# Filter transfers in thirds, networks in three pieces, and A's last Haar products behind C's first pieces

## The chip, the cores and the metric

One core of one Trainium2 chip (the record numbers the chips of the three batches of experiments 1, 3 and 4; each batch has its own runs of the kernel before). The time is the device time of one launch in microseconds (us), given as the median of several runs. Every run told of here was in the fast state, and every kernel's result agreed with the reference. The engines: PE is TensorE, PEld its weight loads, DVE VectorE, ACT ScalarE, POOL GpSimd, SP the engine that issues the transfers. Half clock means that the profile shows a granted clock of PE of 0.5.

## The reference, cut to what matters

Four layers in fp32 on x of (4, 64, 256, 256). Layers 0, 2 and 3 are long convolutions whose filters come from a small network; layer 1 mixes channels in the Haar domain.

```python
def implicit_filter(z, ...):                 # z: 256 positions x 33
    h = sin(freq * (z @ w1 + b1)); h = sin(freq * (h @ w2 + b2)); h = sin(freq * (h @ w3 + b3))
    return (h @ wo) * decay                  # 256 x 64: one filter of 256 taps per channel
def conv(x, ...):                            # layers 0, 2, 3
    hx, hy = implicit_filter(... X ...), implicit_filter(... Y ...)
    k = outer product of hx and hy per channel
    y = irfft2(rfft2(x, 512) * rfft2(k, 512) / 512)[..., :256, :256]   # a causal 2-D convolution
    return y + x * bias[:, None, None]
def haar_layer(x, v, conv_w, tau):           # layer 1
    f = haar2d(x)
    acc = sum_i soft_threshold(einsum("bchw,oc->bohw", f * v[i], conv_w[i]), tau[i])    # i = 0, 1
    return haar2d(acc, inverse=True) + x
```

## The kernel before

The filter is an outer product, so each convolution is a Toeplitz product along the rows and one along the columns. The program has three phases on two groups of two images. **A** is layer 0 and the forward Haar transform; its coefficients go to DRAM (`coef`). **B** mixes them and stores `mixed`. **C** is the inverse Haar transform and layers 2 and 3. B reads the coefficients back into `ft`, mixes them on PE (into a tile that is called `f` too) and thresholds them through `m`; in C the inverse Haar transform goes through `ci`, whose products with a Haar matrix on PE are `c1ps` and give `cz`; the row and column products of layer 2 are `c1r` and `c1c`, those of layer 3 `c2r` and `c2c`. A has 64 rounds of 12 pieces; in a round PE does four products with rows (`a1ps`), four with columns (`a2ps`) and the Haar products of the round before (`a3ps`). PE's schedule is the program's order; other engines receive their work in that order too.

A Toeplitz tile is read from DRAM. For that each filter is written 24 times, padded with zeros to a period of 384, into `filt`. This is `spread`: for one layer and one quarter of the channels, two DMAs (X filter, Y filter) of 16 source rows each.

```python
PERIOD, REPEATS = N + P, 24            # 384 elements, 1536 bytes a repeat
...
    def network(ls):                   # the networks of the layers ls, as pieces
        def front(d):
            ...                        # one matmul and one eviction to u per layer
            nc.vector.tensor_scalar(k, u, INV_2PI, ROUND, ALU.mult, ALU.add)
            nc.vector.tensor_scalar(k, k, ROUND, None, ALU.subtract)
            for c in (C1, C2, C3):
                nc.vector.scalar_tensor_tensor(u, k, -c, u, ALU.mult, ALU.add)
            nc.vector.tensor_scalar(u, u, PI, -PI, ALU.min, ALU.max)
        def back():
            nc.scalar.activation(st["h"], st["u"], AF.Sin)
        ...
        for d in range(3):
            pieces += [lambda d=d: front(d), back]
    ...
    def spread(l, q):
        begin = q * QUARTER if (l, q) != (0, 0) else FIRST * CI
        for w in range(2):
            s = slice(w * C + begin, w * C + (q + 1) * QUARTER)     # 16 rows
            src = filters[l][s].unsqueeze(1)
            nc.sync.dma_start(filt[l][s], src.to_broadcast([src.shape[0], REPEATS, PERIOD]))
    ...
    rest = [load_tau] + [lambda q=q: spread(0, q) for q in range(1, 4)]
    rest.append(...)                                                # weights of two networks
    rest += network([1, 2])
    rest += [lambda l=l, q=q: spread(l, q) for l in (1, 2) for q in range(4)]
    rest.append(scale_tau)
```

The list `rest` lies beside the first 32 rounds of A, evenly over its pieces:

```python
    def beside(main, side, lead, tail):
        done = 0
        for k, p in enumerate(main):
            p()
            want = len(side) * max(0, k + 1 - lead) // max(1, len(main) - lead - tail)
            for q in side[done:want]:
                q()
            done = max(done, want)
    ...
    beside(a[:cut_a], rest, 2, 3 * M)                               # M = 4
```

The end of a round's data: GpSimd makes the Haar transform along the free axis into `fw`; PE multiplies half of it by a Haar matrix (`product`) and transposes the other half, which DVE transforms (in tiles `t`; from round 31 on PE multiplies all of it); ACT moves the products to `f`. `f` has two buffers, and its stores go to `coef`. All transfers are issued by SP.

```python
        def product(t, j):
            if j == 0:
                s["f"] = big("out", f"f_{t}", 2)      # two buffers
            ...
            later(lambda: nc.scalar.activation(dst, ps, AF.Copy, scale=wcol_sb[:, m : m + 1]))
        def store(t):
            for e in range(CI):
                nc.sync.dma_start(coef[grp][c0 + e], src)            # 512 KB each
```

A meets C here. `a_last[0]` is the rest of GpSimd's work on the last round, `a_last[1:M+1]` its Haar products, `c_first` the first inverse Haar products, and `c[:M]` the first row products (`c1r`) of C.

```python
    beside(a[-6 * M : -2 * M], c_before[:1], 2 * M, M)
    beside(a[-2 * M :], c_before[1:], 0, 0)           # first inverse Haar of C, on DVE
    main = a_last[:1] + c_first
    for pair in zip(c[:M], a_last[1:]):
        main += pair
    main += a_last[M + 1 :] + c[M:cut_c]
    beside(main, phase_b(1), 5 * M, 0)
```

Of the kernel before, what the change touches and what calls it, by code (L numbers as in the profile page):

```python
# [48 lines left out]
PERIOD = N + P  # L49
REPEATS = 24  # L50
# [6 lines left out]
M = CI * NB  # L57
# [15 lines left out]
def conv_haar_kernel(  # L73
    ctx: ExitStack, tc: tile.TileContext, x, zT, w1, wbd, cols, decay, wo_first, decay_first, bias, haarW, haarH, ident, wcol, wrow, mixT, v, tau, out
):
    nc = tc.nc
# [8 lines left out]
    filt = [dram.tile([P, REPEATS, PERIOD], F32, tag=f"filt{l}", name=f"filt{l}") for l in range(NL)]  # L85
# [26 lines left out]
    def load_toeplitz(l, t, bufs):  # L112


        tiles = []
        for e in range(CI):
            c = t % ROUNDS * CI + e
            tile_ = image("toep", f"toep{l}_{t}_{e}", bufs)
            for w in range(2):
                start = (w * C + c) * REPEATS * PERIOD  # L120
                src = bass.AP(filt[l].tensor, filt[l].offset + start, [[PERIOD - 8, 16], [PERIOD - 1, 8], [1, N]])
                nc.sync.dma_start(tile_[:, w, :], src)
            tiles.append(tile_)
        return tiles
# [8 lines left out]
    def constant(name, src, shape):  # L133
        t = mp.tile(shape, F32, tag=name, name=f"{name}_sb")
        nc.sync.dma_start(t, src)
        return t
# [9 lines left out]
    def network(ls):  # L146

        n = len(ls)
        st = {}

        def part(name, width=N, bufs=1):
            return mp.tile([P, n, width], F32, tag=f"{name}{n}", name=f"{name}{ls[0]}", bufs=bufs)

        def front(d):
            ps = mps.tile([P, n, N], F32, tag="ps", name=f"mlp_ps{ls[0]}{d}")
            u, k = part("u"), part("k")
            for e, l in enumerate(ls):
                if d == 0:
                    nc.tensor.matmul(ps[:, e, :], w1_sb[:, l, :], z_sb[:, l, :], start=True, stop=True)
                else:  # L160
                    nc.tensor.matmul(ps[:, e, :], wbd_sb[l][:, d - 1, :], st["h"][:, e, :], start=True, stop=True)
            for e, l in enumerate(ls):
                nc.vector.tensor_scalar(
                    u[:, e, :], ps[:, e, :], cols_sb[:, l, d : d + 1], cols_sb[:, l, 3:4], ALU.add, ALU.mult
                )

            nc.vector.tensor_scalar(k, u, INV_2PI, ROUND, ALU.mult, ALU.add)
            nc.vector.tensor_scalar(k, k, ROUND, None, ALU.subtract)
            for c in (C1, C2, C3):
                nc.vector.scalar_tensor_tensor(u, k, -c, u, ALU.mult, ALU.add)  # L170
            nc.vector.tensor_scalar(u, u, PI, -PI, ALU.min, ALU.max)
            st["u"] = u

        def back():
            st["h"] = part("h", bufs=2)
            nc.scalar.activation(st["h"], st["u"], AF.Sin)

        def repeated(r):

            ps = mps.tile([4 * REPEATS, N], F32, tag="ps", name=f"mlp_first{r}")  # L180
            nc.tensor.matmul(ps, wo_first_sb[:, r], st["h"][:, 0], start=True, stop=True)
            t = repeats[r]
            nc.vector.tensor_tensor(t[:, :N], ps, decay_first_sb[:, r], ALU.mult)
            for w in range(2):
                to = filt[0][w * C + r * CI : w * C + (r + 1) * CI].rearrange("c r e -> (c r) e")
                nc.sync.dma_start(to, t[w * CI * REPEATS : (w + 1) * CI * REPEATS])


        def last():
            ps = mps.tile([P, n, N], F32, tag="ps", name=f"mlp_out{ls[0]}")  # L190
            for e, l in enumerate(ls):
                nc.tensor.matmul(ps[:, e, :], wbd_sb[l][:, 2, :], st["h"][:, e, :], start=True, stop=True)
            padded = part("padded", PERIOD)
            nc.vector.memset(padded, 0.0)
            for e, l in enumerate(ls):
                nc.vector.tensor_tensor(padded[:, e, :N], ps[:, e, :], decay_sb, ALU.mult)
                filters[l] = padded[:, e, :]

        pieces = []
        for d in range(3):  # L200
            pieces += [lambda d=d: front(d), back]
        if ls == [0]:
            pieces += [lambda r=r: repeated(r) for r in range(FIRST)]
            pieces += [lambda r=r: first_toep.append(load_toeplitz(0, r, 4 * CI)) for r in range(FIRST)]
        return pieces + [last]
# [5 lines left out]
        nc.gpsimd.memset(t, 0.0)  # L211
    QUARTER = C // 4

    def spread(l, q):

        begin = q * QUARTER if (l, q) != (0, 0) else FIRST * CI
        for w in range(2):
            s = slice(w * C + begin, w * C + (q + 1) * QUARTER)
            src = filters[l][s].unsqueeze(1)
            nc.sync.dma_start(filt[l][s], src.to_broadcast([src.shape[0], REPEATS, PERIOD]))  # L220

    thresholds = []

# [27 lines left out]
    for p in network([0]):  # L251
        p()

    rest = [load_tau] + [lambda q=q: spread(0, q) for q in range(1, 4)]
    rest.append(lambda: wbd_sb.extend(constant(f"wbd{l}", wbd[:, l], [P, 3, P]) for l in (1, 2)))
    rest += network([1, 2])
    rest += [lambda l=l, q=q: spread(l, q) for l in (1, 2) for q in range(4)]
    rest.append(scale_tau)

    def toeplitz(ps, data, t, which):  # L260
# [61 lines left out]
    def phase_a():  # L322
# [138 lines left out]
        def piece(t, j):  # L461
            flush()
            if j == 0:
                if t == 0:
                    load(0)
                    load(1)
                    spread(0, 0)
                load(t + 2)
            if j < M:
                rows(t, j)  # L470
                if t > 0:
                    run(st[t - 1]["ops"], 2)
            elif j < 2 * M:
                columns(t, j - M)
                if j == M and t > 1:
                    coarsest(t - 2)
                if j == M + 2 and t > 1 + paired:
                    store(t - 2)
            else:
                if j == 2 * M and 1 < t <= 1 + paired:  # L480
                    store(t - 2)
                if t > 0:
                    product(t - 1, j - 2 * M)
                if t < total - 1:
                    run(st[t]["ops"], 2)
            if j == 3 * M - 1 and 0 < t <= paired:
                run(st[t - 1]["pair"], 2)
            if j < 2 * M and 1 < t <= 1 + paired:
                run(st[t - 2]["pair"], 2)
# [284 lines left out]
# [10 lines that stand above are left out]
    (a, a_last), (c_before, c_first, c) = phase_a(), phase_c()  # L784
    cut_a, cut_c = ROUNDS * 3 * M, (ROUNDS - 2) * 4 * M
# [6 lines left out]
    beside(a[cut_a : -6 * M], phase_b(0), 5 * M, 0)  # L792
    beside(a[-6 * M : -2 * M], c_before[:1], 2 * M, M)
    beside(a[-2 * M :], c_before[1:], 0, 0)
    main = a_last[:1] + c_first
    for pair in zip(c[:M], a_last[1:]):
        main += pair
    main += a_last[M + 1 :] + c[M:cut_c]
    beside(main, phase_b(1), 5 * M, 0)
    during.close()  # L800
    wp = pool("w", 2)
# [109 lines left out]
```

## Time and profile before

The median of four runs is 2908.59 us (2906.88 to 2909.84); the profiled run's span is 2905.2 us. The rows below take the start of a round as its first `a1ps` matmul in the timeline. An undisturbed round of this phase is 13.14 us long, or 14.00 us when it also holds matmuls of a network; from round 31 on, with all Haar products on PE, it takes about 14.05 us (rounds 32 and 33).

| stretch of PE's time, before | us | lost in it |
|---|---|---|
| start to the first A matmul | 23.5 | not touched |
| rounds 0 to 7 | 107.0 | first transfers, layer 0 |
| rounds 8 to 17 | 140.4 | 5.5 over 10 x 13.14 and four network matmuls of 0.87 |
| rounds 18 to 33 | 233.0 | rounds 25, 28 and 31 took 19.5, 21.0 and 19.9 |
| rounds 34 to 61, beside group 0's mixing | 651.0 | not touched |
| round 62 to the first `c2r` matmul | 55.5 | wait for `fw`, half clock |
| the rest (C, group 1's mixing) | 1694.7 | not touched |

The view that the prediction leaves out is that of the transfers. These are before's while the filters of layers 1 and 2 are written; the columns of the last two lines are the tile, the number of DMAs, the size of one and the median time from issue to landing. The first two lines are forty equal slices of the window: tenths of busy time of the 16 DMA engines, and what they moved.

```profile
DMA  7998899889999988887899989998879998899887
GB/s 279 262 154 154 248 261 328 110 130 274 330 314 146 141 270 274 140 165 181 271 340 331 144 113 210 296 196 130 142 262 267 371 242 119 127 316 270 138 165 221
...
coef<-f SPq DMA_DIRECT2D x23, 512.0 KB, 12.2
filt<-padded SPq DMA_DIRECT2D x16, 576.0 KB, 8.4
```

Read the first line against the second. The engines are busy everywhere, yet eight times the rate falls to between 110 and 165 GB/s: eight pairs of filter transfers. A busy engine isn't a fast one.

### The profile page before, as it was taken

How to read it: one execution, taken by the hardware profiler on the slowest of the kernel's cores; microseconds unless marked ns; L12 is line 12 of the kernel's file. 1: busy time of each engine (PE TensorE's matmuls, PEld its weight loads, DVE VectorE, ACT ScalarE, POOL GpSimd, SP SyncE). 2: the span in 40 equal slices, each digit the busy share in tenths (PEclk: the TensorE clock that was granted, in tenths of full speed). 3: DMA queues.
4: the chain of work that ended last, by engine and by line, in shares of the span. 5: the costliest groups of instructions: out<-in, count | busy, mean ns of one | idle time of the engine just before them, and what ended most of it. 6: DMA issues, size and time to landing. Idle time of an engine off the chain costs nothing.

```text
span 2905.2 us, 46908 instructions
## 1 busy us (share of the span) xinstructions
PE 2837.1 (98%) x16428; PEld 2413.6 (83%) x16428; DVE 1968.5 (68%) x3461; ACT 1141.9 (39%) x1731; POOL 1955.6 (67%) x2486
## 2 busy tenths in 40 slices
PE   7999989999999999999999999999999999999999
PEld 6989978777777777888888888888899999999998
DVE  4577643888888887377777777777755666656665
ACT  2344333555555555344444444444422122221221
POOL 4777766888888888666676676676684455544550
PEclk9999999999999999999999999999999999999999
DMA  7966998999999997686777777777644444444442
GB/s 194 231 202 199 214 221 245 340 327 318 319 309 326 323 312 270 217 279 225 262 263 240 259 250 259 241 257 257 209 144 150 146 135 131 137 149 147 135 131 80
DMA packets 372697, 657.66 MB, mean 226 GB/s; under 512 B 33742, under 2 KB 273775, under 8 KB 372464
## 3 DMA queue, kind: packets, MB, share of 16 engines
q1 hardware_dynamic: 372464, 654.67, 70.0%
q8 instruction: 132, 2.16, 0.3%
q14 instruction: 101, 0.83, 0.1%
HBM read 438.53 MB, written 216.01 MB: 225 GB/s over the span
## 4 chain that ended last, share of the span: by engine, by line
PE 81%; DVE 6%; DMA 4%; POOL 3%; issue 3%; ACT 2%; SPq 0%; DVEq 0%; POOLq 0%; ACTq 0%
PE f L536 12%; PE c2c L264 8%; PE c1r L264 8%; PE c1c L264 8%; PE c2r L264 8%; PE a1ps L264 5%; PE a2ps L264 5%; PE c2c L265 4%; PE c2r L265 4%; PE c1c L265 4%; PE c1r L265 4%; PE a3ps L372 3%; PE a1ps L265 2%; PE a2ps L265 2%; PE wps L661 2%
## 5 line engine op out<-in xcount | busy, mean ns | idle before, releaser
L544 ACT ACTIVATE m<-f 128x1024 f32<-128x1024 f32 x256 | 262.2, 1024 | 639.3 <-DVE f L540 595.6
L536 PE MATMUL f<-ft,mix_sb 128*128 128x512 f32 x1024 | 489.2, 600 | 21.6 <-DVE m L554 21.0
L551 DVE TENSOR_TENSOR f<-f,tau 128x1024 f32<-128x1024 f32 x256 | 314.9, 1230 | 166.0 <-ACT f L547 166.0
L559 POOL TENSOR_TENSOR m<-m,ft 128x1024 f32<-128x1024 f32 x128 | 302.2, 2361 | 179.5 <-DVE m L554 179.0
L562 POOL TENSOR_TENSOR gt<-m,m 128x1024 f32<-128x1024 f32 x128 | 302.1, 2360 | 157.4 <-DVE m L554 138.7
L540 DVE TENSOR_TENSOR f<-f,v 128x1024 f32<-128x1024 f32 x256 | 314.6, 1229 | 120.2 <-PE f L536 118.8
L264 PE MATMUL a1ps<-toep,x 128*128 128x256 f32 x1024 | 312.4, 387 | 17.7 <-ACT f L381 14.4
L554 DVE SCALAR_TENSOR_TENSOR m<-f,m 128x1024 f32<-128x1024 f32 x256 | 311.0, 1215 | 0.0
L264 PE MATMUL c2c<-toep,ch 128*128 128x256 f32 x1024 | 306.3, 381 | 0.0
L264 PE MATMUL a2ps<-toep,ay 128*128 128x256 f32 x1024 | 305.9, 381 | 0.1
L264 PE MATMUL c2r<-toep,cy 128*128 128x256 f32 x1024 | 305.8, 380 | 0.0
L264 PE MATMUL c1c<-toep,ch 128*128 128x256 f32 x1024 | 305.8, 380 | 0.0
L536 PEld LDWEIGHTS f<-ft,mix_sb 128*128 128x128 f32 x1024 | 174.5, 190 | 154.7 <-issue 122.4
L696 ACT COPY ch<-c2r 128x512 f32<-128x512 f32 x256 | 149.9, 588 | 357.6 <-PE c2r L265 356.6
L696 ACT COPY ch<-c1r 128x512 f32<-128x512 f32 x256 | 148.5, 589 | 328.2 <-PE c1r L265 328.1
L547 ACT ACTIVATE f<-f 128x1024 f32<-128x1024 f32 x256 | 263.0, 1027 | 0.0
L710 DVE SCALAR_TENSOR_TENSOR o<-cy,bias_sb,c2c 128x512 f32<-128x512 f32 x256 | 188.8, 742 | 71.1 <-PE c2c L265 64.7
L352 DVE SCALAR_TENSOR_TENSOR x<-x,bias_sb,a2ps 128x512 f32<-128x512 f32 x256 | 188.1, 743 | 65.0 <-PE a2ps L265 48.0
L299 POOL TENSOR_TENSOR i<-g 128x8 f32<-128x8 f32 x63 | 13.5, 215 | 322.3 <-DMA g<-mixed 322.2
L381 ACT ACTIVATE f<-a3ps,wcol_sb 128x512 f32<-128x512 f32 x196 | 130.7, 684 | 253.4 <-PE a3ps L372 145.0
L299 POOL TENSOR_TENSOR i<-i,g 128x16 f32<-128x16 f32 x378 | 205.9, 545 | 26.0
L273 POOL TENSOR_TENSOR fw<-x 128x1024 f32<-128x1024 f32 x64 | 121.2, 1894 | 148.9 <-DVE x L352 148.6
(97 smaller groups left out, 6600.1 us busy)
## 6 DMA issues: line engine op xcount, KB each, us to landing
toep<-filt SPq DMA_DIRECT2D x768, 128.0 KB, 3.4
x<-in_x SPq DMA_DIRECT2D x256, 256.0 KB, 6.1
coef<-f SPq DMA_DIRECT2D x128, 512.0 KB, 4.2
ft<-coef SPq DMA_DIRECT2D x128, 512.0 KB, 6.0
v<-in_v SPq DMA_DIRECT2D x128, 512.0 KB, 6.7
tau<-taus SPq DMA_DIRECT2D x128, 512.0 KB, 6.6
mixed<-gt SPq DMA_DIRECT2D x128, 512.0 KB, 4.9
g<-mixed SPq DMA_DIRECT2D x128, 512.0 KB, 6.3
```

The costliest lines, as they stand in the source:

```text
L264: nc.tensor.matmul(ps[:, m, :], data[:, 0, cut], t[:, which, :], start=True, stop=False)
L265: nc.tensor.matmul(ps[:, m, HALF:], data[:, 1, cut], t[:, which, :HALF], start=False, stop=True)
L299: engine.tensor_tensor(even, s, d, ALU.add)
L536: nc.tensor.matmul(un[u]["f4"][:, j, :], mix_sb[:, u % 2, :], f[:, j, :], start=True, stop=True)
L540: nc.vector.tensor_tensor(f4, f4, weights(st[u // 2]["v"], u % 2), ALU.mult)
L544: nc.scalar.activation(un[u]["m"], un[u]["f4"], AF.Sign)
L547: nc.scalar.activation(un[u]["f4"], un[u]["f4"], AF.Abs)
L551: nc.vector.tensor_tensor(f4, f4, weights(st[u // 2]["tau"], u % 2), ALU.subtract)
L554: nc.vector.scalar_tensor_tensor(un[u]["m"], un[u]["f4"], 0.0, un[u]["m"], ALU.max, ALU.mult)
L559: nc.gpsimd.tensor_tensor(m0, m0, data(st[s]["f"]), ALU.add)
L562: nc.gpsimd.tensor_tensor(data(st[s]["g"]), m0, un[2 * s + 1]["m"], ALU.add)
L696: later(lambda: nc.scalar.copy(y, ps))
```

## The change

Its intent: shorter bursts of filter traffic, so that the stores of `f` don't wait behind them; a network's arithmetic out of the way of DVE's evictions; and other work for PE while GpSimd finishes the last `fw`.

```diff
-        def front(d):
+        def product(d):
             ...                                  # matmuls, evictions to u
+            st["u"], st["k"] = u, k
+        def reduce():
+            u, k = st["u"], st["k"]
             nc.vector.tensor_scalar(k, u, INV_2PI, ROUND, ALU.mult, ALU.add)
             ...                                  # the other five instructions, as before
-        def back():
+        def sine():
             ...
-            pieces += [lambda d=d: front(d), back]
+            pieces += [lambda d=d: product(d), reduce, sine]
...
-    def spread(l, q):
+    def spread(l, q, part=slice(0, REPEATS)):
             ...
-            nc.sync.dma_start(filt[l][s], src.to_broadcast([src.shape[0], REPEATS, PERIOD]))
+            times = part.stop - part.start
+            nc.sync.dma_start(filt[l][s, part], src.to_broadcast([src.shape[0], times, PERIOD]))
...
-    rest = [load_tau] + [lambda q=q: spread(0, q) for q in range(1, 4)]
+    thirds = [slice(k, k + REPEATS // 3) for k in range(0, REPEATS, REPEATS // 3)]
+    rest = [load_tau] + [lambda q=q, k=k: spread(0, q, k) for q in range(1, 4) for k in thirds]
...
-    rest += [lambda l=l, q=q: spread(l, q) for l in (1, 2) for q in range(4)]
+    rest += [lambda l=l, q=q, k=k: spread(l, q, k) for l in (1, 2) for q in range(4) for k in thirds]
...
-    main = a_last[:1] + c_first
-    for pair in zip(c[:M], a_last[1:]):
+    main = a_last[:1] + c_first + c[:M]
+    for pair in zip(c[M : 2 * M], a_last[1:]):
         main += pair
-    main += a_last[M + 1 :] + c[M:cut_c]
+    main += a_last[M + 1 :] + c[2 * M : cut_c]
```

The list `rest` grows from 21 to 46 items, so the spacing changes with the size: the transfers not only get smaller, they also begin earlier. The two aren't the same cause, and the experiments take them apart.

More of the change, by code (lines that the diff above doesn't have):

```diff
@@ L171, in front @@
             nc.vector.tensor_scalar(u, u, PI, -PI, ALU.min, ALU.max)
-            st["u"] = u
-        def back():
+        def sine():
             st["h"] = part("h", bufs=2)
```

## The prediction

> **What bounds the kernel now.** I read the page's busy row first, then the busy times by stretch, then TensorE's waits, then the timeline around the longest ones. The page says that TensorE (PE) is the bound nearly everywhere:
>
> ```profile
> PE 2837.1 (98%) x16428; PEld 2413.6 (83%) x16428; DVE 1968.5 (68%) x3461; ACT 1141.9 (39%) x1731; POOL 1955.6 (67%) x2486
> ```
>
> The change adds no matmul and removes none, so it can only gain PE's idle time, 2905.2 - 2837.1 = 68.1 us, and what half-clock matmuls cost after an idle stretch. The stretches show where that lies (columns: window, its length, busy time and count of each engine, granted PE clock, DMA share, GB/s):
>
> ```profile
> 24.00:140.00 116.00, 114.85 (x735) 106.20 (x735) 57.90 (x146) 42.08 (x78) 80.01 (x149) 1.00 0.89 227
> 140.00:260.00 120.00, 115.99 (x770) 107.84 (x769) 87.89 (x204) 49.72 (x91) 89.53 (x155) 1.00 0.63 203
> 260.00:355.00 95.00, 95.00 (x636) 88.88 (x635) 59.41 (x154) 39.00 (x72) 72.92 (x137) 1.00 0.85 217
> 355.00:470.00 115.00, 101.22 (x638) 93.61 (x637) 56.29 (x153) 36.99 (x71) 73.57 (x147) 0.94 0.90 221
> ...
> 504.00:1150.00 646.00, 624.35 (x3162) 468.30 (x3161) 517.89 (x492) 367.45 (x477) 566.18 (x652) 1.00 0.92 319
> ...
> 1185.00:1205.00 20.00, 14.85 (x86) 14.09 (x87) 3.59 (x9) 5.75 (x11) 18.76 (x33) 0.83 0.48 157
> ```
>
> The reader should see: 13.8 us idle and a clock of 0.94 at 355 to 470; 4.0 us idle at 140 to 260; 5.2 us idle and a clock of 0.83 at 1185 to 1205; and 21.7 us at 504 to 1150, where A and the group-0 mixing share the engines, which the change does not touch. The start (17 us until the first convolution) isn't touched either. The waits of PE name the releasers:
>
> ```profile
> PE f L536 <- DVE m L554: 21.0, 38, 1.5
> PE a1ps L264 <- ACT f L381: 14.4, 4, 5.5
> ...
> PE a3ps L372 <- POOL fw L278: 4.8, 2, 4.3
> PE a3ps L372 <- DVE t L436: 4.0, 3, 1.4
> ```
>
> The second row is the large one. ScalarE (ACT) moves the Haar products out of PSUM into f, which has two buffers; it cannot begin before the older f has landed in DRAM. ACT's waits at 340 to 470 and the landing of those stores (the view of tile coef; at 150 to 300 its median was 3.0 us) say so:
>
> ```profile
> ACT f L381 <- DMA coef<-f: 49.4, 5, 14.7
> ```
> ```profile
> DMA to landing us min/median/max: 5.4/12.3/14.9
> ```
>
> PE then stalls when its four PSUM banks are full. The first stall, and the one at the start of C, in PE's timeline:
>
> ```profile
> 370.10 1.22 PE L264 MATMUL a1ps<-toep,x 128*128 128x256 f32 x2 [4.42 <-ACT f L381]
> ```
> ```profile
> 1195.99 2.00 PE L372 MATMUL a3ps<-haarH_sb,fw 128*128 128x128 f32 x8 [4.34 <-POOL fw L278]
> ```
>
> **What the Trainium skill says.** "TensorE: Matmul & The Clock Gate", Part 1 (the HAM clock gate): after about one idle window of 3.4 us the PE clock drops to half and needs a busy window to return. The trace agrees on the half: the 1.22 us above is 0.60 us for the same pair elsewhere. So each long stall costs more than its idle time. "DMA: Bandwidth & Descriptors", Queues, rings and completion order: each DMA engine consumes its descriptors in ring order. The trace agrees: coef stores issued just behind a filter transfer take 12 to 15 us. "TensorE: Matmul & The Clock Gate", Architectural detail: VectorE (DVE) is a strict FIFO, so evictions queue behind a network's arithmetic; the third kind of stall shows that.
>
> **Part 1: filter transfers in thirds.** Side work is spread evenly over the first 384 pieces of A: with a lead of 2 and a tail of 12, one item per 370/21 = 17.6 pieces before, one per 370/46 = 8.04 after (before: 1+3+1+7+8+1 = 21 items; after: 1+9+1+10+24+1 = 46). A round of 12 pieces takes 13.14 us in the timeline (349.75 to 362.89), so an item comes each 19.3 us before, each 8.8 us after. The bytes are the same. What a filter transfer costs the queue I read from landings. The pair issued at 350.75 and 351.39 landed at 358.59 and 365.71; the last Toeplitz tile ahead of it landed at 354.46. So 11.2 us per pair of 576 KB transfers, about 105 GB/s. A round's other transfers (four x, four Toeplitz, two coef) take about 8.1 us when queued back to back (two rounds between 365.71 and about 382). Demand before: 1.47 rounds x 8.1 + 11.2 = 23.1 us per 19.3 us. The queue is overdrawn by 3.8 us each time, 8 times: 30 us. Rounds 25, 28 and 31 are longer than 13.14 us by 6.3, 7.9 and 6.8 us: 21.0 us lost, idle and half clock together; the buffers absorbed the other 9. Demand after: 0.67 x 8.1 + 11.2/3 = 9.1 us per 8.8 us, 24 times: overdrawn by about 7 us in all, which is within the 9 us that the buffers absorbed. And a coef store stands behind 3.7 us of filter instead of 11.2. I expect 21.0 us to shrink to about 3. The same at 60 to 130, where three bursts cost one round 1.2 us: gain 1.
>
> The 48 more transfers at about 0.6 us issue each are 29 us of the SP queue over some 370 us; it is not on the path.
>
> **Part 2: networks in smaller pieces.** Before, a layer's two evictions (1.0 us) and six arithmetic instructions (4.9 to 5.6 us) sit in DVE's order in one block, behind the first two instructions of the transposed Haar pair, which wait for ACT. At 147.39 to 153.46 the block delays the evictions of a2ps; PE waits 1.42, 1.29 and 1.30 us. The rounds concerned are longer by 1.76, 1.52 and 1.54 us: 4.8 us. After, the instruction order shows the evictions some eight pieces earlier and the arithmetic ahead of the Haar pair. DVE was idle for 2.94 us just there, so the delay falls from about 6 to about 2.7 us; stall = delay - 5.2 us by the first case (L352 4.6 us late, 1.42 us stalled, so only some 3.2 us of lateness is free), and nothing is left. Gain 4.5.
>
> **Part 3: A's last Haar products behind C's first pieces.** Before, PE does one c1r piece and then waits until 1195.99 for fw from GpSimd (POOL). After, three more c1r pieces and one c1c piece come first: 4 x 1.31 = 5.2 us of work from 1191.65, to 1196.9, later than fw's end at 1195.95. Their inputs exist: DVE wrote the last cz at 1191.59. So the 4.34 us goes, and with it the half clock behind it (2.00 for 1.06, 1.06 for 0.60, 0.63 for 0.38 and 0.83 for 0.60: about 1.7 us on the path). The wait of 2.30 us at 1185.81 for DVE ci stays. POOL's last coefficients come four small operations later, 0.8 us, so the last coef store goes at about 1209.4 instead of 1208.51, and the first ft lands near 1218.6. The first mixing matmul would start at 1226.25 - 6 = 1220.2: it still fits. Gain 6.0, less 0.5 for that narrow margin.
>
> **Sum.** 18 + 1 + 4.5 + 5.5 = 29 us; 2908.5 - 29 = 2880 us, 1.0% faster.
>
> **Rivals.** (a) The stall stays since bytes, not bursts, set it. For: the DMA share is already 0.90 to 0.92 from 280 on, and 9.1 of 8.8 us is no real slack; if a third has its own fixed cost of 0.5 us, the deficit is 19 us and some 8 to 10 us of stall return. Against: at 280 to 355 PE lost nothing under the same share, and the transfers now begin near 220 us instead of 287, when the share was 0.63. It would give 2888 to 2892. (b) Part 3 turns into a wait for ft or for ci of the next rounds, since POOL is busy 18.76 of 20 us there. Against: POOL's next ci ends at 1207.87 and PE needs it at 1217.04 - 6 = 1211. It would give 2884 to 2886. (c) Transfers that start at 42 us meet the first loads of x and make a new stall at the start (DMA share 0.73 to 0.93 there): 2882 to 2885. (d) All stalls of parts 1 to 3 vanish, and with fewer cold phases: 21.0 + 1.2 + 4.8 + 6.0 = 33 us, 2875.
>
> **Range and chances.** The best is 2875, with 2 us for the free phase of the clock's window below it; (a) and (b) together give about 2893. So 2873 to 2893 holds 8 in 10. Faster by over 2% would need 58 us, nearly all of PE's loss, of which 22 us in group-0 mixing and 17 us at the start are untouched: 1%. Slower by over 2% has no mechanism: 1%.
>
> **What would show it.** Right: no PE wait over 2 us for ACT f at 350 to 470, granted clock 0.98 or more there, coef landings mostly under 9 us at a DMA share still near 0.9; the three waits for DVE t gone; the wait for POOL fw at C's start gone, and PE busy for 17 or more of the 20 us there. Part 1 is wrong if rounds near the end of the transfers are still over 15 us long with coef landings of 12 us; part 2 if the waits for DVE come back at other rounds; part 3 if a new wait for ft, ci or cz stands within 30 us behind. PE f L536 waiting for DVE m should stay at about 21 us; if it moves by more than 4 us, the side effects are larger than I allow.

## The result and the profile after

The changed kernel took 2878.42 us (median of four runs, 2878.32 to 2879.07) against 2908.59. A ratio here is the mean time of one kernel's fast runs over the mean of the other's fast runs in the same rounds, so not quite the ratio of these medians: 0.9897, 95% interval 0.988 to 0.9914. The prediction, 2880 with a range of 2873 to 2893, holds. PE's busy time fell by only 9.6 us of half-clock matmuls (2837.1 - 2827.5); the rest of the 28.5 us of span (2905.2 - 2876.7) was idle time.

This is the busy row of the page after:

```profile
PE 2827.5 (98%) x16428; PEld 2406.8 (84%) x16428; DVE 1981.4 (69%) x3461; ACT 1146.2 (40%) x1731; POOL 1960.6 (68%) x2486
```

The stretches after, with the same columns as in the prediction; the windows after 355 are shifted by the gain:

```profile
140.00:260.00 120.00, 116.75 (x777) 108.96 (x776) 94.88 (x201) 50.83 (x93) 93.20 (x158) 1.00 0.66 201
...
355.00:450.00 95.00, 94.89 (x637) 88.86 (x636) 59.59 (x151) 38.48 (x70) 72.55 (x136) 1.00 0.76 228
...
480.00:1125.00 645.00, 623.04 (x3157) 467.20 (x3156) 515.94 (x490) 366.92 (x477) 565.65 (x649) 1.00 0.95 320
...
1159.00:1176.00 17.00, 14.70 (x98) 13.97 (x97) 8.02 (x15) 6.67 (x13) 12.94 (x28) 0.90 0.59 198
```

At 355 to 450 PE is idle for 0.1 us in 95 and the clock is full; before, it lost 13.8 us there. At 140 to 260 it still loses 3.3 us, where 4.0 went before: little was gained. Beside group 0's mixing, 480 to 1125, the 22.0 us of idle time stayed, and at C's start, 1159 to 1176, 2.3 us of idle time and a clock of 0.90 remain of 5.2 and 0.83. PE's waits after say the same with names (time in all, how often, the longest):

```profile
PE f L541 <- DVE m L559: 21.3, 38, 1.5
...
PE a3ps L377 <- DVE t L441: 3.2, 3, 1.1
...
PE c1ps L644 <- DVE ci L306: 2.3, 1, 2.3
```

The row for ACT `f` (14.4 us) is gone, so is that for POOL `fw` at C's start, and the row for DVE `t` has lost 0.8 us of 4.0. The transfers after, in the corresponding window:

```profile
coef<-f SPq DMA_DIRECT2D x34, 512.0 KB, 3.1
...
filt<-padded SPq DMA_DIRECT2D x48, 192.0 KB, 4.4
```

A coefficient store lands in 3.1 us where 12.2 were needed, 5.4 at the longest. From the starts of the rounds in the two timelines, the whole difference can be told:

| stretch | before, us | after, us | difference |
|---|---|---|---|
| to the first A matmul | 23.51 | 23.61 | +0.1 |
| rounds 0 to 7 | 107.01 | 104.84 | -2.2 |
| rounds 8 to 17, over undisturbed rounds | 5.51 | 4.32 | -1.2 |
| rounds 18 to 33 | 233.04 | 213.72 | -19.3 |
| rounds 34 to 61 | 651.02 | 651.32 | +0.3 |
| round 62 to the first `c2r` | 55.51 | 49.26 | -6.2 |
| the rest | 1694.72 | 1694.74 | 0.0 |

The sum is 28.5 us, that of the spans. The medians differ by 30.2: the profiled execution of the kernel before took 2906.99 us, 1.6 less than the median.

### The profile page after: what moved, and what is told of

Read it like the earlier page. It is cut to its first block, busy times and chain, and to the rows that moved or that the text cites. A ratio compares the mean times of both kernels' runs of the same rounds, so it can differ in the third digit from the quotient of the medians.

```text
span 2876.7 us, 46942 instructions
## 1 busy us (share of the span) xinstructions
PE 2827.5 (98%) x16428; PEld 2406.8 (84%) x16428; DVE 1981.4 (69%) x3461; ACT 1146.2 (40%) x1731; POOL 1960.6 (68%) x2486
## 4 chain that ended last, share of the span: by engine, by line
PE 84%; DVE 6%; issue 3%; DMA 2%; ACT 2%; POOL 1%; SPq 0%; DVEq 0%; ACTq 0%; POOLq 0%
PE f L541 12%; PE c2c L269 8%; PE c1r L269 8%; PE c2r L269 8%; PE c1c L269 8%; PE a1ps L269 6%; PE a2ps L269 5%; PE c2c L270 4%; PE c2r L270 4%; PE c1c L270 4%; PE c1r L270 4%; PE a3ps L377 3%; PE a1ps L270 3%; PE a2ps L270 3%; DVE f L545 2%
## 5 line engine op out<-in xcount | busy, mean ns | idle before, releaser
L541 PE MATMUL f<-ft,mix_sb 128*128 128x512 f32 x1024 | 489.1, 600 | 22.0 <-DVE m L559 21.3
L357 DVE SCALAR_TENSOR_TENSOR x<-x,bias_sb,a2ps 128x512 f32<-128x512 f32 x256 | 188.2, 743 | 67.9 <-PE a2ps L270 48.6
L278 POOL TENSOR_TENSOR fw<-f 128x512 f32<-128x512 f32 (+6 forms) x448 | 198.0, 442 | 29.4
```

The lines of the kernel that those rows point to most:

```text
L541: nc.tensor.matmul(un[u]["f4"][:, j, :], mix_sb[:, u % 2, :], f[:, j, :], start=True, stop=True)
```

## The experiments

Ten kernels, in three batches; each batch has its own runs of the kernel before, whose median was 2906.37, 2907.73 and 2907.92 us.

| run | median, us | of before (95%) |
|---|---|---|
| thirds only, at the old pace | 2884.74 | 0.9925 (0.9909 to 0.9942) |
| change, but whole transfers | 2883.32 | 0.9923 (0.9906 to 0.994) |
| last products only | 2899.51 | 0.9974 (0.9966 to 0.9983) |
| change, network block whole, early | 2877.25 | 0.99 (0.9885 to 0.9915) |
| before, 128 source rows | 2887.21 | 0.9929 (0.9914 to 0.9943) |
| before, 64 source rows | 2887.17 | 0.9931 (0.9914 to 0.9947) |
| change, arithmetic cut up | 2874.59 | 0.9886 (0.9871 to 0.9901) |
| all together | 2872.52 | 0.9879 (0.9864 to 0.9893) |
| all together, products later | 2871.57 | 0.9877 (0.986 to 0.9893) |
| change, network block whole, late | 2879.77 | 0.9904 (0.9889 to 0.9918) |

**Part 1: the size or the pace.** My theory was the burst: a store of `f` stands behind a long filter transfer. The rival was the balance of work per time, which the new spacing alone could mend. The first kernel takes the thirds at the old mean pace (each old item has three slots; the middle third of a quarter goes out where the whole quarter did, the others a third of the old spacing before and behind it); the second takes the change's pace with whole transfers.

```diff
 # thirds only, at the old pace: on the kernel before
+    rest = [none] * (3 * len(slots))          # slots: the old list of 21 items
+            for n, k in enumerate(thirds):
+                rest[3 * at + 1 + n] = lambda item=item, k=k: spread(*item, k)
 # whole transfers at the new pace: on the changed kernel
-    rest += [lambda l=l, q=q, k=k: spread(l, q, k) for l in (1, 2) for q in range(4) for k in thirds]
+    rest += [p for l in (1, 2) for q in range(4) for p in (none, lambda l=l, q=q: spread(l, q), none)]
```

> The kernel before with nothing changed but this: each filter transfer is cut into three, and the three go out at one third, two thirds and three thirds of the old spacing, so pace, window and bytes are those of before (11 transfers of 1.2 MB, one per 19.3 us). Networks and the last products are as before. Theory (a transfer in pieces costs the queue less: the mean 1536-byte packet takes 122 ns in the changed kernel against 180 ns in the one before): the queue's demand falls from 23.1 to about 19.5 us per 19.3 us, the three long rounds of A (21 us lost) shrink to under 4 us, coef stores land in under 8 us at the median: 2887 to 2892 us. Rival (pace, not size, mattered: the changed kernel spreads the same bytes over 211 us instead of 155): the queue stays overdrawn, at least 12 of the 21 us remain: 2899 to 2909 us.

> The changed kernel, but every filter transfer is whole again and takes the middle one of the three places that its thirds had (two empty places around it): the pace and the window of the changed kernel with the bursts of the one before. Theory (size matters): packets back at about 180 ns, a coef store behind a burst lands after 12 us or more, and 4 to 12 us of PE waits for ACT f with their half-clock stretches come back: 2883 to 2892 us. Rival (pace alone): no wait over 2 us at 200 to 450, 2877 to 2880 us, the same as the changed kernel.

The transfers of the kernel with thirds at the old pace, while the filters are written, with the two lines of slices first:

```profile
DMA  8989899999979989899999989989997996898897
GB/s 159 277 207 294 190 314 238 260 311 264 266 236 267 327 194 276 209 298 313 250 296 307 275 267 308 266 175 339 305 203 287 283 255 184 271 315 201 296 310 195
...
coef<-f SPq DMA_DIRECT2D x22, 512.0 KB, 3.5
filt<-padded SPq DMA_DIRECT2D x46, 192.0 KB, 4.5
```

And those of the kernel with whole transfers at the new pace:

```profile
coef<-f SPq DMA_DIRECT2D x30, 512.0 KB, 11.8
...
filt<-padded SPq DMA_DIRECT2D x15, 576.0 KB, 8.0
```

With thirds at the old pace the 16 rounds from 18 on took 213.4 us, as after the change (213.7). The DMA engines were as busy as before (a share of 0.91 while the filters were written, in both kernels), and the stores landed in 3.5 us instead of 12.2. So the DMA share said nothing here, and the balance of work per time was not the cause. What moved is the rate: before spends 16 of its 40 slices under 170 GB/s, this kernel one, and its mean there is 262 GB/s instead of 221. The size alone suffices; the time, 2884.74 us, is even below the 2887 to 2892 that I had expected.

But the pace alone nearly suffices too. With whole transfers every 27 us or so instead of every 22, the stores still land in 11.8 us and ACT still waits for them (39.4 us in all in the view of tile `coef`, 49.4 before), yet PE loses only 1.8 us in two waits near the end (0.65 for ACT `f`, 1.19 put down to DVE `t`). Of the 4 to 12 us of waits for ACT `f` that I had expected there were 1.2 in the whole run. Rounds 18 to 33 took 216.0 us, 2.2 more than after the change. The medians are 4.9 us apart (2883.32 against 2878.42), but half of that isn't the transfers' doing as far as is shown: round 9 took 16.9 us instead of 14.5, since a wait for DVE `t` behind a network's arithmetic (1.86 us instead of 1.10) was followed by 3.4 us at half clock; the last filter transfer before it had been issued some 40 us earlier. I read this so: a slow store harms PE only when the next one comes before the buffers have recovered. The size is the cure that removes the slow store, the pace only makes it bearable. PE at the end of round 9, with whole transfers at the new pace and after the change:

```profile
156.59 3.03 PE L378 MATMUL a3ps<-haarH_sb,fw 128*128 128x128 f32 x16 [1.86 <-DVE t L442]
```
```profile
154.58 2.02 PE L377 MATMUL a3ps<-haarH_sb,fw 128*128 128x128 f32 x16 [1.10 <-DVE t L441]
```

**Why a filter transfer is slow.** A whole item is 1.18 MB (2 x 16 rows x 24 x 1536 bytes). From the trace's packet records, first start to last end, it took 11.5 to 14.0 us before: 92 GB/s at the mean of 12.8. The Trainium skill, "SBUF — State Buffer", section "Door 1: The DMA port swizzle", says that what a DMA reaches depends on its partitions: 16 neighbouring partitions reach 4 of 16 ports, measured there at 104 GB/s, 64 reach 8 at 196, and 128 reach all at 328. The 92 GB/s are near the page's 104, as if the two halves of an item went one after the other. If so, the same bytes from more source rows with fewer repeats should take less time at the old pace and the old size:

```diff
 # on the kernel before; 64 rows: two DMAs of 64 rows in place of one of 128
+    def wide(l, q):
+        part = slice(6 * q, 6 * q + 6)
+        for s in (slice(0, P),):
+            src = filters[l][s].unsqueeze(1)
+            nc.sync.dma_start(filt[l][s, part], src.to_broadcast([src.shape[0], 6, PERIOD]))
-    rest += [lambda l=l, q=q: spread(l, q) for l in (1, 2) for q in range(4)]
+    rest += [lambda l=l, q=q: wide(l, q) for l in (1, 2) for q in range(4)]
```

> The kernel before with one edit: for layers 1 and 2 the same 1.2 MB per item at the same pace goes out as one transfer from all 128 partitions with six repeats each, instead of two transfers of 0.6 MB from 16 partitions with 24 repeats each. So the single transfer is twice as large as before and six times as large as a third. Theory[...]: the mean filter packet falls from 180 to under 90 ns, coef stores land in under 6 us, the long rounds 25, 28 and 31 lose under 2 us in all: 2885 to 2888 us. Rival (size of a burst on the ring is what counts): coef stores still 10 us or more behind the bigger burst and at least 10 us of stall: 2895 to 2910 us.

> As the run with 128 rows, but two transfers of 0.6 MB, from partitions 0 to 63 and 64 to 127, six repeats each[...]. Theory (ports): the pair takes about half of the 11 to 13 us that it takes before, packets 90 to 130 ns, stalls in A's last rounds under 4 us: 2885 to 2891 us. Rival (size): as before, 2902 to 2909 us.

The transfers with 128 source rows, then with 64:

```profile
coef<-f SPq DMA_DIRECT2D x20, 512.0 KB, 2.9
...
filt<-padded SPq DMA_DIRECT2D x7, 1152.0 KB, 6.5
```

```profile
coef<-f SPq DMA_DIRECT2D x22, 512.0 KB, 3.0
...
filt<-padded SPq DMA_DIRECT2D x15, 576.0 KB, 6.6
```

An item of unchanged bytes took 3.7 to 4.8 us from 128 rows (274 GB/s at 4.3 us) and 5.5 to 6.2 us from 64 (199 GB/s at 5.9), after 92 GB/s from 16. The order and roughly the sizes are the page's (328, 196, 104). The mean 1536-byte packet took 68 and 91 ns, where before's took 180. No round was long any more (213.3 us for rounds 18 to 33 in both), though a transfer of 1152 KB is twice the largest one before. So it was neither the size nor the pace that made the stores wait: it was the time during which a transfer from 16 rows holds the queue, and thirds are one way to shorten that. One rival within this reading is untested: rows and repeats changed together (16 x 24, 64 x 6, 128 x 6), and only the step from 64 to 128 keeps the repeats, so reading the same row 24 times may have a part in the slowness from 16 rows.

That both kernels are 2.5 us slower than thirds at the old pace lies elsewhere in the traces. Layer 0's filters are still whole there, and a wait for ACT `f` of 0.5 and 1.3 us stands in round 8, some 20 us behind the last of them. At C's start the wait for `ci` was not followed by half clock, so PE came earlier to `fw` and waited 6.0 us for it instead of 4.3, with 6.8 us at half clock behind that wait instead of 3.4.

One thing isn't explained. A third from the same 16 rows took 3.3 us on average after the change (2.3 to 4.7), less than a third of 12.8, and its mean packet 122 ns. That short transfers let the two halves of an item overlap on different ports is argued only; no run shows it.

**Part 3 alone.**

```diff
 # on the kernel before: only the main list of the change
+    main = a_last[:1] + c_first + c[:M]
+    for pair in zip(c[M : 2 * M], a_last[1:]):
```

> The kernel before with part 3 alone (A's last Haar products behind C's first four pieces). Theory: the wait of 4.34 us for POOL fw and the half clock behind it (1.7 us) go, nothing replaces them: 6.0 to 6.4 us faster, 2902 to 2903 us. Rival (a new wait for ft or ci takes its place): 2904 to 2908 us with a wait of over 1 us within 40 us behind.

2899.51 us, 6.9 less than before's 2906.37 in the same batch (6.0 to 6.4 were expected), whose runs spread over 2901.7 to 2913.2; the traces give a firmer number. From round 62 to the first `c2r` it took 49.26 us, exactly as after the change (55.51 before): 6.25 us. No wait for `ft`, `ci` or `fw` took the place of the one removed. The sum of the two parts measured alone, 21.6 (2906.37 - 2884.74) and 6.9, is 28.5 us, and with 1.2 for part 2 it is 29.7, where the change brought 30.2: as far as these medians can tell, the parts don't depend on each other.

**Part 2: what became of the networks' arithmetic.** I had expected the waits for DVE `t` to vanish. This is DVE's timeline before, at the first network layer (start, length, the last figure how many instructions):

```profile
148.41 1.20 DVE L167 TENSOR_SCALAR k<-u 128x512 f32<-128x512 f32 x1
149.64 0.72 DVE L168 TENSOR_SCALAR k<-k 128x512 f32<-128x512 f32 x1
150.39 2.60 DVE L170 SCALAR_TENSOR_TENSOR u<-k,u 128x512 f32<-128x512 f32 x3
153.03 0.43 DVE L171 TENSOR_SCALAR u<-u 128x512 f32<-128x512 f32 x1
```

And after the change:

```profile
141.05 0.42 DVE L171 TENSOR_SCALAR k<-u 128x512 f32<-128x512 f32 x1
141.50 2.00 DVE L172 TENSOR_SCALAR k<-k 128x512 f32<-128x512 f32 x1
143.53 5.16 DVE L174 SCALAR_TENSOR_TENSOR u<-k,u 128x512 f32<-128x512 f32 x3
148.72 0.72 DVE L175 TENSOR_SCALAR u<-u 128x512 f32<-128x512 f32 x1
```

The same six instructions take 8.3 us (0.42 + 2.00 + 5.16 + 0.72) instead of 4.95. GpSimd's timeline after shows what runs beside them:

```profile
141.21 2.01 POOL L278 TENSOR_TENSOR fw<-x 128x1024 f32<-128x1024 f32 x1 [3.74 <-DVE x L357]
143.18 2.07 POOL L283 TENSOR_TENSOR f<-x 128x1024 f32<-128x1024 f32 x1
```

These are the two longest instructions of GpSimd's Haar transform. The tensor_scalar at 141.50 ends at 143.50, just after GpSimd's first one (143.22), and is 2.00 us long where one alone is 0.43. The Trainium skill, "SBUF — State Buffer", section "Who interferes with whom", says that a DVE instruction with two SBUF inputs contends with a GpSimd instruction that reads SBUF, and that tensor_scalar can too in a two-port mode; whichever issues first blocks the other for its whole length. The trace agrees: the change moved the arithmetic to where GpSimd's wide instructions run.

Two kernels put the arithmetic back in one block with the evictions, at the place of the change's product (beside small GpSimd instructions) and at that of its reduce:

```diff
 # on the changed kernel; early, then late
-            pieces += [lambda d=d: product(d), reduce, sine]
+                pieces += [lambda d=d: (product(d), reduce()), lambda: None, sine]
+                pieces += [lambda: None, lambda d=d: (product(d), reduce()), sine]
```

> The changed kernel, but each layer of the second network is one block on VectorE again (two evictions and six arithmetic instructions), at the place of the evictions, eight pieces earlier than the arithmetic stands in the changed kernel; sine stays where it is. Theory (the place counts, not the cut: in the changed kernel the arithmetic took 8.2 us since it ran beside GpSimd's 128x1024 operations[...], and 5 to 6 us elsewhere): the six instructions take under 6 us here and the three waits of 1.1 us for DVE t go or fall under 0.5 us: 2875 to 2878 us. Rival (the cut counts: a block of 8 delays evictions by more than a block of 6): waits of 1.3 us or more come back: 2879 to 2881 us.

> The changed kernel with each layer's block whole again, at the place where the changed kernel has the arithmetic (the tenth piece of the round). With the whole block eight pieces earlier (2877.3 us) this separates the cut from the place. Theory (place): the six instructions stand beside GpSimd's large ones and take 7 us or more, with the evictions ahead of them the lateness is about 1 us more than in the changed kernel: three waits of 1.5 to 2.3 us, 2879.5 to 2883 us. Rival (the cut matters little and the place too): within 1 us of the changed kernel, 2877.5 to 2879.5 us.

DVE with the early block, the first layer:

```profile
135.54 0.43 DVE L171 TENSOR_SCALAR k<-u 128x512 f32<-128x512 f32 x1
136.00 0.43 DVE L172 TENSOR_SCALAR k<-k 128x512 f32<-128x512 f32 x1
136.46 2.14 DVE L174 SCALAR_TENSOR_TENSOR u<-k,u 128x512 f32<-128x512 f32 x3
138.63 0.47 DVE L175 TENSOR_SCALAR u<-u 128x512 f32<-128x512 f32 x1
```

3.5 us for the six: 0.71 for a scalar_tensor_tensor, 1.72 after the change. That half of the theory holds. But the waits did not vanish as I had expected: PE still waited 0.35, 0.97 and 1.07 us for DVE (1.10, 1.07 and 1.07 after the change), and the rounds were 3.5 us over instead of 4.3. In the second layer the block (with its evictions 162.89 to 167.48) now stood inside the Haar steps, and the first of the round's four evictions of `a2ps` came only at 168.19. The late block missed both ways: I had expected at least 7 us of arithmetic and got 5.6 to 5.7, since the evictions ahead of it, which waited for PE, pushed it past GpSimd's widest instructions (in the first layer these ended at 143.7, and the arithmetic began at 143.87); and the waits, expected at 1.5 to 2.3 us, were 1.28, 1.34 and 1.33 us, longer than after the change with its 8.3 us of arithmetic. So the length of the arithmetic alone doesn't set the wait. My reading is that what stands directly ahead of the evictions does, and that a block of 3.5 us is already too long at the wrong place.

The test of that cuts the block: the two tensor_scalar four pieces after the product, the three scalar_tensor_tensor twelve pieces after it, the clip with the sine.

```diff
 # on the changed kernel
-            pieces += [lambda d=d: product(d), reduce, sine]
+                pieces += [lambda d=d: product(d), (turns, None, subtract), lambda: (clip(), sine())]
+    # an item that is a tuple goes to the half slots before and behind its own
```

> The changed kernel with the second network's arithmetic in three parts, placed where GpSimd runs its small operations: two tensor_scalar, three scalar_tensor_tensor, then the clip just ahead of the sine. Theory (the lateness of an eviction is the length of the block ahead of it[...]): the six instructions take 3.4 to 4.5 us in all, no wait of PE for DVE t over 0.3 us, A shorter by 3.5 to 4.3 us: 2874 to 2875 us. Rival (DVE is simply full in these rounds): waits of 0.7 us or more remain: 2876 to 2879 us.

DVE with the arithmetic cut up, the first layer:

```profile
139.64 0.42 DVE L175 TENSOR_SCALAR k<-u 128x512 f32<-128x512 f32 x1
140.09 0.43 DVE L176 TENSOR_SCALAR k<-k 128x512 f32<-128x512 f32 x1
149.81 2.35 DVE L182 SCALAR_TENSOR_TENSOR u<-k,u 128x512 f32<-128x512 f32 x3
154.84 0.42 DVE L187 TENSOR_SCALAR u<-u 128x512 f32<-128x512 f32 x1
```

The sum is 3.6 us, no piece is longer than 2.35, and PE doesn't wait for DVE `t` at all. Rounds 8 to 17 were 0.5 us over the undisturbed ones (4.3 after the change): 3.8 us gained over the change in the traces (2876.7 - 2872.9), and 5.0 over the kernel before, where the prediction had 4.5 for part 2. This kernel changed places as well as cutting; a whole block of 3.5 us at some third place was not tried.

**A version that beats both.** The last kernels add the filters of layers 1 and 2 from 128 rows, and start C's first inverse Haar transform earlier, in small buffers of its own, against the 2.30 us wait for `ci`. The last one also places A's products two pieces further behind.

```diff
 # on the kernel with the arithmetic cut up
+    rest += [p for l in (1, 2) for q in range(4) for p in (lambda: None, lambda l=l, q=q: wide(l, q), lambda: None)]
-    beside(a[-6 * M : -2 * M], c_before[:1], 2 * M, M)
-    beside(a[-2 * M :], c_before[1:], 0, 0)
+    beside(a[-6 * M : -3 * M], c_before[:1], 0, M)
+    beside(a[-3 * M :], c_before[1:], 0, M)
 # and in the last kernel, behind = M + 2 in place of M
+    main = a_last[:1] + c_first + c[:behind]
+    for pair in zip(c[behind : behind + M], a_last[1:]):
```

> The run before plus two things: layers 1 and 2 of the filters from 128 partitions in one transfer each, and C's first inverse Haar transform begun some eight pieces earlier on VectorE, in small buffers of its own, so that it does not wait for GpSimd's forward transform to free them. Theory: the wait of 2.3 us for DVE ci at C's start and the half clock behind it (1.7 us) go: 2870 to 2872 us. Rival (DVE and GpSimd hold each other up[...], the forward transform of A's last but one round comes late): a wait for POOL fw of 1 us or more takes its place: 2873 to 2877 us.

> The last version (arithmetic in parts, filters from 128 partitions, C's first inverse sooner) with A's last Haar products behind six of C's first pieces instead of four, 2.6 us of TensorE work later. Theory: the wait of 2.24 us for POOL fw that came up there goes, nothing else changes: 2870 to 2871 us. Rival (the last coef store and with it the first ft of group 1 come too late): a wait for ft of 1 us or more: 2872 to 2873 us.

PE's waits with all together, without the untouched rows:

```profile
PE f L572 <- DVE m L590: 21.0, 38, 1.5
...
PE a3ps L408 <- POOL fw L314: 2.7, 2, 2.2
```

The wait for `ci` went, and one of 2.24 us for `fw` came: PE got there earlier than GpSimd. From round 62 to the first `c2r` it took 47.6 us, where 49.3 had been needed after the change and 48.6 with the arithmetic cut up. Of the 2.5 us between this trace and that one, 1.0 lies there and 0.4 in rounds 18 to 33; most of the rest is in rounds 0 to 7, which vary anyhow. The rival had named a wait for `fw`, though for another reason. So the median, 2872.52, was just above the range of 2870 to 2872 that I had expected. With the products two pieces further behind:

```profile
PE f L572 <- DVE m L590: 21.0, 38, 1.5
...
PE f L572 <- DMA ft<-coef: 0.5, 1, 0.5
PE a3ps L408 <- POOL fw L314: 0.4, 1, 0.4
```

2871.57 us, just above the expected 2870 to 2871: the wait for `fw` at C's start is gone, and half a microsecond came back as a wait for `ft`, since the last coefficients are stored later. The trace is 1.6 us shorter, but the runs (2870.68 to 2873.2) overlap with those of the version before it (2872.26 to 2873.1), so which of the two is the better stays open. Both are 6 to 7 us under the changed kernel by medians of different batches, at 0.988 of the kernel before. Of PE's waits, those for DVE `m` beside group 0's mixing (21.0 us) and those at the start are what is left.

## Why the prediction was right

The time was right to 1.6 us, and that close by luck: part 2 brought 3.3 us less than predicted, and part 1, part 3 and a variation at the start that the change doesn't explain brought together 3.2 more in the traces; by the medians the gain was 30.2 us where 29 was predicted. By its own steps:

- **What bounds the kernel.** Right: PE's matmuls are unchanged and the gain is its idle time and half-clock time. The untouched waits for DVE `m` stayed (21.0 to 21.3 us), as did the rest of C (1694.7 us in both traces).
- **Part 1, 18 us.** The mechanism (ACT can't begin `f`, since its store waits behind a filter) was right, and so was the size: 19.3 us. The residual of 3 us was 0.7: round 31 took 14.79, of which 14.05 is undisturbed work, since from there on PE makes all the Haar products. For the same reason the loss before was 20.1 us and not 21.0. Of the signs named, the clock (1.00) and the landings (5.4 us at most) came true; the DMA share did not stay near 0.9 but fell to 0.76 at 355 to 450. Its working was less good than its result. By the same balance the thirds at the old pace would have been overdrawn (1.47 x 8.1 + 3 x 3.1 = 21 us per 19.3) and the whole transfers at the new pace more so (2.1 x 8.1 + 13.1 = 30 us per 27); in those rounds the first lost nothing and the second 2.2 us. So the balance, as I had summed it, doesn't tell a kernel that stalls from one that doesn't; the wait behind one transfer does. And 3.7 us for a third was a division by three; 3.3 was measured. The transfers added were 44 (22 items of two), not 48.
- **The further 1 us at 60 to 130.** Not shown. Rounds 0 to 7 were 2.2 us shorter, but the kernel with only part 3, whose transfers there are those of before, has 104.9 us as well. So it varies from run to run.
- **Part 2, 4.5 us.** The step that failed: "so the delay falls from about 6 to about 2.7 us ... and nothing is left". It took the old lengths of DVE's instructions to a new place. There they ran beside GpSimd's widest ones and took 8.3 us, so 1.2 us were gained, and three waits of 1.1 us came back in rounds 9, 11 and 13 in place of 9, 12 and 15, as the prediction's own sign for a wrong part 2 says. Cutting the arithmetic gave another 3.8.
- **Part 3, 5.5 us.** Right, the term slightly small: 6.25 us measured, alone and in the change. The narrow margin for `ft`, for which I had taken off 0.5, cost nothing at this distance; two pieces further it cost 0.5.
- **The rivals.** That bytes and not bursts set the stall (a) fell with the thirds at the old pace: same DMA share, no stall. A new wait behind part 3 (b) did not come with the change; a small one for `ft`, 0.5 us, came with the last kernel. A stall at the start (c) isn't in the trace. The best case (d), 2875, was the kernel with the arithmetic cut up.

The sum is 19.3 + 1.2 + 6.2 = 26.7 us for the parts, and 2 us of variation at the start, where I had 18 + 1 + 4.5 + 5.5.

## What to carry to other kernels

When one queue carries both bulk and urgent transfers, look at how long a single bulk transfer holds it, not at its busy share: let the source span all partitions where it can, and only then cut it or space it out. When instructions move to another place in an engine's order, take their lengths from what will run beside them there, not from where they were. Here a delay in front of evictions was removed by cutting a block into parts that fit between them, not by moving it whole to either of two places.

## What the Trainium skill lacked or had wrong

- "DMA: Bandwidth & Descriptors" doesn't say what a port-bound transfer does to those behind it: a pair from 16 partitions held the queue for 12.8 us, and stores of 512 KB that take 3.1 us landed in 12.2. No page has a number for how well the busy share of the DMA engines hides this: it was 0.91 in two kernels, one in which three rounds lost 20 us (221 GB/s over the window) and one that lost nothing there (262 GB/s).
- "SBUF — State Buffer" has the bandwidth of one large transfer by partitions. Its order held (92, 199 and 274 GB/s for 16, 64 and 128 rows, read from SBUF with each row repeated), but it has nothing for short ones from few partitions: thirds from the same 16 rows took 3.3 us, less than a third of 12.8.
- The same page says who blocks whom on the shared ports, but no page gives the cost in a full pipeline: 0.71 us for a scalar_tensor_tensor of 128x512 beside small GpSimd instructions and 1.72 beside 128x1024 ones; 0.43 and 2.00 for a tensor_scalar.
- "TensorE: Matmul & The Clock Gate" puts the clock's drop at about one idle window of 3.4 us, free-running. An idle time of 2.30 us, the wait for `ci`, was followed by 3.4 us at half clock in the changed kernel and by none in the one with the arithmetic cut up, so a shorter gap suffices in some alignments. The clock records of the traces lie on steps of 3.41 us; of the 2.30 us, 2.2 fell into one step in the changed kernel and 1.7 in the other. With whole transfers at the new pace 1.86 us sufficed, with 64 source rows 1.9 us did not, so where the limit lies stays open. The two lines below, of the changed kernel and of that one, show it in the same pair of matmuls.

```profile
1163.56 0.76 PE L644 MATMUL c1ps<-haarW_sb,ci 128*128 128x128 f32 x2 [2.30 <-DVE ci L306]
```

```profile
1160.34 0.46 PE L668 MATMUL c1ps<-haarW_sb,ci 128*128 128x128 f32 x2 [2.30 <-DVE ci L330]
```
